# Two attention layers on one core: softmax denominators by 32x32 transposes and one product, another choice of moved sums, other buffers

## The chip, the core and the metric

The kernel runs on one core of a Trainium2 chip. Its engines have these names here: PE is TensorE (PEld its weight loads), DVE is VectorE, ACT is ScalarE, POOL is GpSimd, SP is SyncE, which only issues DMAs. The metric is the device time of one launch in microseconds (us), the median of several runs. Each engine works through its own queue of instructions in order, and waits on semaphores for the others.

## The reference

Two self-attention layers follow each other on `x` of shape (4, 64, 64, 256), that is 4 images of N = 4096 tokens with 256 channels. Everything is float32.

```python
# layer 0
q, k, v = x @ Wq + bq, x @ Wk + bk, x @ Wv + bv      # 32, 32 and 256 columns
x = gamma * (softmax(q @ k.T) @ v) + x               # softmax over the keys
# layer 1
f, g, v = x @ Wf + bf, x @ Wg + bg, x @ Wh + bh      # 32, 32 and 128 columns
o = softmax(g @ f.T) @ v
out = x + o @ Wo + bo
```

The kernel takes the exponentials without a maximum and divides by their sum at the end. The change is about that sum, the denominator of each token, in layer 1.

## The kernel before, in words

**Blocks and steps.** The work is a list of `Step(b, l, j, i)`: image b, layer l, block j of queries, step i over the keys. Layer 0 has 16 blocks of 256 queries with 8 steps of 512 keys; layer 1 has 8 blocks of 512 queries with 16 steps of 256 keys. Keys lie on the partitions, so a step's score tile `st` is 128 x 1024. One loop runs over all steps. In each, it issues the scores of the step after next (`later.scores()`), the DVE work of this step and the next, the products of this step, and small units of other work (`run(todo)`) that `plan` has put at fixed steps: projections of the next layer or image, and the `ends` of the block before. The tile framework then arranges the instructions of each engine by times of its own and adds the waits.

**One step.** ACT takes `p = exp(st)` (L544). Steps of layer 0 and the steps `SPLIT1` of layer 1 are split: ACT also makes `high` (L542), DVE makes `low` (L555) and `d` (L560), and PE multiplies each of the three with a part of v at one pass (L582, L600). The other steps of layer 1 multiply the whole `p`, which takes two passes (L600).

**Buffers.** Tiles of one tag share a number of buffers. `wide` makes 128 x 1024 tiles: tag `t` has two (`high`; in layer 1 also the `p` of split steps), `p` three, `l` two, `d` and `e` one each. `d` holds `d` in layer 0 and `p_sum` in layer 1. Tag `small` (128 x 256) has four and serves `x_res`, `x1`, `y` and two tiles of the start. Two PSUM tiles of tag `side` serve all small products: projections, transposes, outputs.

**Denominators of layer 0** come with the products, as a further column of v (W = C + 2).

**Denominators of layer 1.** `add_up` adds the `p` of a block's steps on DVE into `p_sum` (L571, L573), save those in `MOVED_SUMS`, which are added by DMA: the first is copied into `p_sum_moved` (tag `e`, L548), the others are accumulated there (L550), all issued from POOL's queue. `end_second` adds the two (L659), then its two halves (L660 `sums`, 128 x 512). The partitions are still to be summed: in each of the four units `output(t)`, PE takes 128 tokens of `sums` as the stationary operand and multiplies them with a column of ones (L668), beside the output product with Wo (L667) and into the same PSUM tile. DVE takes the reciprocal (L670), ACT scales the output by it (L673), and a DMA of POOL's queue accumulates it into `out` (L675). `plan` puts the four units at steps 1 to 4 of the next block.

**End of a block of layer 0.** `residual(s)`, for two tiles of 128 tokens: DVE makes `x1` (L628), SP writes it to `x1_dram`, POOL adds the last bias into `x_res` (L639), SP writes that to `out` (L640).

**Projections.** `qk_unit` multiplies the two parts of x into a PSUM tile `ps`. ACT copies its lower half into an SBUF tile `whole` (L439), DVE adds the upper half and the bias into `whole` (L440), ACT rounds it into `parts[top]` (L441), DVE takes the rest into `parts[bottom]` (L442), and SP writes `parts` to DRAM. `load_rows` (L493) loads queries and keys from there by POOL's queue; `keys` lists the loads still to come.

**The check at the end.** After the last block, DVE compares all reciprocals in `inverse` and the largest values in `seen_v` with bounds (L808 to L819), PE counts the violations (L821), and a branch (L831) would run a general path.

Of the kernel before, what the change touches and what calls it, by code (L numbers as in the profile page):

```python
# [57 lines left out]
P = 128  # L58
# [10 lines left out]
MOVED_SUMS = (0, 4, 7, 9, 12)  # L69
# [169 lines left out]
def fast_path(ctx: ExitStack, tc: tile.TileContext, x, w0, w1, wo, bo, gamma, out, off):  # L239
# [27 lines left out]
    def wide(tag, name, dtype=F32):  # L267
        return work.tile([P, 2 * QB], dtype, tag=tag, bufs={"d": 1, "e": 1, "p": 3}.get(tag, 2), name=name)
# [41 lines left out]

    inverse = const.tile([P, 2, B * N // P], F32, name="inverse")
# [12 lines left out]
    for l, (q_w, q_b, k_w, k_b, v_w, v_b) in enumerate((w0, w1)):  # L324
        queue = (nc.scalar, nc.gpsimd)[l]
        w_sb = work.tile([P, NCC, 2 * D], F32, tag="small", bufs=4, name=f"wqk_whole{l}")
        b_sb = const.tile([2 * D, 1], F32, name=f"bqk{l}")
        for g, w_dram, b_dram in ((0, q_w, q_b), (D, k_w, k_b)):
            queue.dma_start(w_sb[:, :, g : g + D], w_dram.rearrange("(c p) d -> p c d", p=P))
            queue.dma_start(b_sb[g : g + D, :], b_dram.rearrange("(d o) -> d o", o=1))  # L330
        w_parts = const.tile([P, NCC, 4 * D], F32R, name=f"wqk{l}")
        high, low = w_parts[:, :, : 2 * D], w_parts[:, :, 2 * D :]
        nc.scalar.copy(high, w_sb)
        nc.vector.tensor_sub(low, w_sb, high.bitcast(F32))
        wqk.append(w_parts)
        bqk.append(b_sb)
        v_sb = const.tile([P, NCC, CV[l]], F32, name=f"wv{l}")
        queue.dma_start(v_sb, v_w.rearrange("(c p) d -> p c d", p=P))
        wv.append(v_sb)
# [20 lines left out]
    def bias_units():  # L360


        def issue():
            nc.vector.tensor_scalar(bv, bv, gamma_sb, None, ALU.mult)
            wide_bias = work.tile([P, P], F32, tag="small", bufs=4, name="wide_bias")
# [10 lines left out]
    q_t, moved_sums, first_p, waiting = {}, {}, [], {}  # L376
# [35 lines left out]
    def project_units(b, l, h):  # L412
# [5 lines left out]
        def qk_unit():  # L418
# [10 lines left out]
            whole = data.tile([2 * D, QB0], F32, tag="qk", name=f"qk_{b}_{l}_{h}")  # L429
# [9 lines left out]
            nc.scalar.copy(whole, ps[bottom, :])  # L439
            nc.vector.scalar_tensor_tensor(whole, ps[top, :], bqk[l], whole, ALU.add, ALU.add)  # L440
# [50 lines left out]
    def load_rows(dst, parts, which, order):  # L491
        for n, h in enumerate(order):
            nc.gpsimd.dma_start(dst[n * D : (n + 1) * D, :], parts[h, which])  # L493
# [16 lines left out]
    def small(name):  # L510
        return work.tile([P, C], F32, tag="small", bufs=4, name=name)


    class Step:
# [8 lines left out]
        def scores(self):  # L523
# [19 lines left out]
            self.p = wide("t" if self.split and l == 1 else "p", f"p_{self.key}")  # L543
            nc.scalar.activation(self.p, s_flat, AF.Exp)  # L544
            if l == 1 and i in MOVED_SUMS:
                if i == MOVED_SUMS[0]:
                    moved_sums[b, j] = wide("e", f"p_sum_moved_{b}_{j}")
                    nc.gpsimd.dma_start(moved_sums[b, j], self.p)  # L548
                else:
                    nc.gpsimd.dma_start(moved_sums[b, j], self.p, accum_op=ALU.add)  # L550
# [13 lines left out]
        def add_up(self, p_sum):  # L564
# [5 lines left out]
            elif self.i == kept[1]:  # L570
                nc.vector.tensor_add(p_sum, first_p.pop(0), self.p)  # L571
            else:
                nc.vector.tensor_add(p_sum, p_sum, self.p)  # L573
# [80 lines left out]
    def end_second(b, j, acc, p_sum, o):  # L654
        key = f"{b}_{j}"
        for h in range(QB // QB0):
            nc.vector.tensor_add(o[h][:, :QB0], o[h][:, :QB0], acc[1][:, h * QB0 : (h + 1) * QB0])
        sums = work.tile([P, QB], F32, tag="sums", bufs=1, name=f"sums_{key}")
        nc.vector.tensor_add(p_sum, p_sum, moved_sums[b, j])  # L659
        nc.vector.tensor_add(sums, p_sum[:, :QB], p_sum[:, QB:])  # L660

        def output(t):
            def issue():
# [4 lines left out]
                nc.tensor.matmul(ps[:, C : C + 1], sums[:, tok], ones[:, :1], start=True, stop=True)  # L668
                n = (b * N + j * QB) // P + t
                nc.vector.reciprocal(inverse[:, 1, n : n + 1], ps[:, C : C + 1])  # L670
# [8 lines left out]
        return [output(t) for t in range(NT)]  # L679

    def run(units):
        for u in units:
            u()

# [15 lines left out]
    acc, p_sum, units = None, None, {}  # L700

    def plan(b, l, j, ends):
# [20 lines left out]
        else:  # L723
            for n, u in enumerate(ends):
                put(1 + n, u)
        if b + 1 < B:
# [8 lines left out]
    for n, s in enumerate(steps):  # L735
        b, l, j = s.b, s.l, s.j
        if s.first:
# [5 lines left out]
            if l == 1:  # L743
                p_sum = wide("d", f"p_sum_{b}_{j}")
# [24 lines left out]
        s.add_up(p_sum)  # L769
# [31 lines left out]
        if s.last:  # L801
            ends = end_first(b, j, acc) if l == 0 else end_second(b, j, acc, p_sum, o)
    run(ends)

    good = small("good").rearrange("p (l n) -> p l n", l=2)
    nc.vector.tensor_scalar(good, inverse, 1.0 / SUM_MAX, None, ALU.is_ge)  # L808
    nc.vector.tensor_scalar(inverse, inverse, 1.0 / SUM_MIN, None, ALU.is_le)
    nc.vector.tensor_mul(good, good, inverse)  # L810
    nc.vector.tensor_scalar(seen_v, seen_v, VALUE_MAX, None, ALU.is_le)
    size = const.tile([P, 1], F32, name="size")
    nc.vector.tensor_mul(size, gamma_sb, gamma_sb)
    nc.vector.tensor_scalar(size, size, GAMMA_MAX**2, None, ALU.is_le)
    low = const.tile([P, 1], F32, name="low")
    for seen, axes in ((good, AX.XY), (seen_v, AX.XY)):
        nc.vector.tensor_reduce(low, seen, axes, ALU.min)
        nc.vector.tensor_mul(size, size, low)
# [54 lines left out]
```

## Time and profile before

| What | Value |
|---|---|
| Median of 3 runs | 3158.69 us (3158.46 to 3160.62) |
| Profiled execution, its own time | 3155.92 us |
| Span of its profile | 3154.1 us |
| Granted TensorE clock | 0.998 |
| ACT: p (L544), 1024 times | 1042.5 us, 1021 ns each |
| DVE: low (L555), 704 times | 936.6 us, 1330 ns each |
| DVE: p_sum added (L573), 288 times | 352.6 us, 1224 ns each |
| DVE: transposes of x (L392), 112 times | 79.0 us, 705 ns each |
| PE: whole p (L600), 1280 passes | 611.0 us, 597 ns each |
| DMA: p into p_sum_moved, 160 issues | 512 KB each, 4.7 us to landing |

The page shows one execution. A row of a group gives line, engine, operation, what it writes and reads, shape, count, then busy time and mean duration, then the idle time of the engine just before and what ended it. Matmuls are pipelined and their ends are modelled, so on PE the distance from one start to the next says more than a duration. A row of the order in time gives start, duration, engine, line, operation, and how many were merged. "Passes" are PE instructions: a product of float32 operands is two of them, each with its own weight load; one of fp32r operands is one.

### The profile page before, as it was taken

To read this page: it belongs to the slowest core of one execution; us is meant where nothing else is said; L and a number is where in the kernel's file an instruction comes from. 1 tells how busy PE (TensorE), PEld (TensorE's weight loads), DVE (VectorE), ACT (ScalarE), POOL (GpSimd) and SP (SyncE) were. 2 spreads that over 40 slices of the span, in tenths; PEclk is the share of its full clock that TensorE was granted. 3 is DMA by queue.
4 is the path that set the end of the run, shared out by engine and by line. 5 is a ranking of instruction groups with operands and counts; after the bars stand their busy time and mean duration, and the time that the engine had idled before them with its cause. 6 is when DMAs were issued, how large, how long until landed. Compare 5 with 4: busy or idle time off the path is not lost.

```text
span 3154.1 us, 54090 instructions
## 1 busy us (share of the span) xinstructions
PE 3116.3 (99%) x19908; PEld 2672.0 (85%) x19908; DVE 2689.1 (85%) x3237; ACT 2140.1 (68%) x2835; POOL 900.7 (29%) x1108
## 2 busy tenths in 40 slices
PE   8999999999999999999999999999999999999997
PEld 7999998666799999866679999976668999996664
DVE  7888888888888888888888888898888888888876
ACT  7666666777666666777766666677776666666674
POOL 5232224222422222422242222232223222233221
PEclk9999999999999999999999999999999999999999
DMA  4121114555512121555541112255554111125454
GB/s 119 43 53 47 48 48 104 107 108 105 104 44 51 41 53 47 113 101 112 107 93 47 49 45 51 51 116 107 105 113 81 48 46 47 49 65 105 97 95 73
DMA packets 391392, 239.49 MB, mean 76 GB/s; under 512 B 266672, under 2 KB 355248, under 8 KB 391120
## 3 DMA queue, kind: packets, MB, share of 16 engines
q0 software_dynamic: 68160, 134.86, 22.0%
q1 hardware_dynamic: 322048, 100.76, 13.4%
q8 instruction: 161, 2.64, 0.4%
q14 instruction: 111, 0.91, 0.1%
q10 hardware_dynamic: 912, 0.33, 0.1%
HBM read 82.58 MB, written 67.11 MB: 47 GB/s over the span
## 4 chain that ended last, share of the span: by engine, by line
PE 91%; DVE 3%; DMA 2%; issue 2%; ACT 1%; POOL 0%; SPq 0%; DVEq 0%; ACTq 0%; POOLq 0%
PE acc L600 24%; PE acc L582 23%; PE acc_pair L582 23%; PE st L532 14%; PE psv L464 4%; PE psqk L422 2%; PE pso L667 2%; DVE d L560 1%; DVE low L555 1%; ACT p L544 1%; DVE p_sum L573 1%; DMA p_sum_moved<-p 0%; DMA squares<-in_x 0%; PE pso L668 0%; DMA squares<-x_dram 0%
## 5 line engine op out<-in xcount | busy, mean ns | idle before, releaser
L542 ACT ACTIVATE high<-st,down 128x1024 fp32r<-128x1024 f32 x704 | 786.5, 1117 | 703.2 <-PE st L532 362.8
L544 ACT ACTIVATE p<-st 128x1024 f32<-128x1024 f32 x1024 | 1042.5, 1021 | 166.3 <-PE st L532 143.8
L560 DVE SCALAR_TENSOR_TENSOR d<-low,high 128x1024 fp32r<-128x1024 f32 x704 | 871.0, 1237 | 227.0 <-PE acc_pair L582 223.7
L555 DVE TENSOR_TENSOR low<-p,high 128x1024 fp32r<-128x1024 f32 x704 | 936.6, 1330 | 142.6 <-ACT p L544 141.6
L532 PE MATMUL st<-q,k 128*128 128x256 f32 (+1 forms) x3072 | 706.3, 338 | 2.5 <-DMA k<-qk_parts 1.4
L600 PE MATMUL acc<-p,v 128*128 128x512 f32 x1280 | 611.0, 597 | 0.0
L532 PEld LDWEIGHTS st<-q,k 128*128 128x128 f32 x3072 | 470.0, 189 | 103.3 <-issue 40.6
L639 POOL TENSOR_TENSOR x_res<-x,bo 128x256 f32<-128x256 f32 x128 | 212.5, 1660 | 879.3 <-DVE x L628 879.2
L600 PEld LDWEIGHTS acc<-p,v 128*128 128x128 f32 x1280 | 233.1, 189 | 161.8 <-issue 143.4
L573 DVE TENSOR_TENSOR p_sum<-p_sum,p 128x1024 f32<-128x1024 f32 x288 | 352.6, 1224 | 9.4 <-ACT p L544 5.8
L582 PE MATMUL acc<-v0h,high 128*128 128x258 f32 x2048 | 341.6, 284 | 1.2 <-ACT high L542 1.2
L582 PE MATMUL acc<-v0d,d 128*128 128x258 f32 x2048 | 339.2, 287 | 2.6 <-DVE d L560 2.2
L582 PE MATMUL acc<-v0l,low 128*128 128x256 f32 (+1 forms) x2048 | 329.3, 283 | 0.6 <-DVE low L555 0.5
L582 PE MATMUL acc_pair<-v0h,high 128*128 128x258 f32 x2048 | 329.8, 283 | 0.0
L582 PE MATMUL acc_pair<-v0l,low 128*128 128x256 f32 (+1 forms) x2048 | 328.8, 282 | 0.0
L582 PE MATMUL acc_pair<-v0d,d 128*128 128x258 f32 x2048 | 328.5, 282 | 0.0
L582 PEld LDWEIGHTS acc<-v0h,high 128*128 128x128 f32 x2048 | 286.0, 189 | 3.1 <-issue 1.4
L582 PEld LDWEIGHTS acc<-v0d,d 128*128 128x128 f32 x2048 | 281.5, 190 | 5.6 <-DVE d L560 4.9
L582 PEld LDWEIGHTS acc<-v0l,low 128*128 128x128 f32 x2048 | 282.2, 190 | 1.8 <-DVE low L555 1.3
L582 PEld LDWEIGHTS acc_pair<-v0h,high 128*128 128x128 f32 x2048 | 282.1, 189 | 0.0
L582 PEld LDWEIGHTS acc_pair<-v0l,low 128*128 128x128 f32 x2048 | 281.1, 189 | 0.0
L582 PEld LDWEIGHTS acc_pair<-v0d,d 128*128 128x128 f32 x2048 | 281.0, 189 | 0.0
(108 smaller groups left out, 3332.5 us busy)
## 6 DMA issues: line engine op xcount, KB each, us to landing
p_sum_moved<-p POOLq DMA_DIRECT2D x160, 512.0 KB, 4.7
x_res<-in_x SPq DMA_DIRECT2D x128, 128.0 KB, 2.1
qk_dram<-qk_parts SPq DMA_DIRECT2D x128, 128.0 KB, 1.9
x_dram<-x SPq DMA_DIRECT2D x128, 128.0 KB, 1.7
out<-x_res SPq DMA_DIRECT2D x128, 128.0 KB, 1.7
squares<-x_dram SPq DMA_DIRECT2D x512, 32.0 KB, 1.9
out<-y POOLq DMA_DIRECT2D x128, 128.0 KB, 3.2
q<-qk_dram POOLq DMA_DIRECT2D x252, 64.0 KB, 2.2
```

The lines of the kernel that those rows point to most:

```text
L422: nc.tensor.matmul(ps, wqk[l][:, c, :], x_parts[key][n][:, c, :], start=(c == n == 0), stop=(c == NCC - 1 and n == 1),)
L464: nc.tensor.matmul(ps[:, t, :], xT[key][:, c, t * P : (t + 1) * P], wv[l][:, c, :], start=(c == 0), stop=(c == NCC - 1),)
L532: nc.tensor.matmul(st[:, g, :], k_t[b, l, kt // NT][:, kt % NT * P : (kt % NT + 1) * P], q_t[b, l, j * n // QB][:, q0 : q0 + n], start=Tru ...
L542: nc.scalar.activation(self.high, s_flat, AF.Exp, bias=down)
L544: nc.scalar.activation(self.p, s_flat, AF.Exp)
L555: nc.vector.tensor_sub(self.low, self.p, self.high.bitcast(F32))
L560: nc.vector.scalar_tensor_tensor(self.d, self.low.bitcast(F32), -UP, self.high.bitcast(F32), ALU.mult, ALU.add)
L573: nc.vector.tensor_add(p_sum, p_sum, self.p)
L582: nc.tensor.matmul(acc[2 * s + which][:, :width], p[:, g * QB0 + s * P : g * QB0 + (s + 1) * P], v0[self.i][v][:, g, :width], start=self.f ...
L600: nc.tensor.matmul(acc[which], v_part[:, g, :], p[:, g * QB : (g + 1) * QB], start=first and g == 0, stop=last and g == G[1] - 1,)
L639: nc.gpsimd.tensor_add(x_old[s], x_new[s], bo_sb)
L667: nc.tensor.matmul(ps[:, :C], part, wo_sb, start=True, stop=True)
```

## The change

Six edits stand in the diff.

1. **Denominators.** For all blocks of layer 1 but the very last, the four products with ones go. A unit `turn` transposes the 32x32 blocks of `sums` on DVE into the other half of `p_sum` and sums each run of 32, which gives `part_sums`, 128 x 16. A unit `denominators` multiplies it on PE with `same`, a constant with ones where two partitions agree modulo 32, into a side tile `psd` of 16 columns, and takes four reciprocals of 32 x 4. The two units stand ahead of the four outputs, so the ends of a block are six units, at steps 1 to 6 of the next. `same` is built on POOL at the start.
2. **Moved sums.** The steps are (3, 4, 6, 7, 9, 12) and not (0, 4, 7, 9, 12). The `p` of the first, step 3, is made in the tag-`e` buffer itself, so nothing is copied; five are accumulated there. `tc.issue_after(loads[0].ins)` keeps each behind the last load of `load_rows` in POOL's queue. `p_sum` is taken at the second kept step and no longer at the block's first.
3. **Buffers.** Tag `t` has three, `small` has three and not four, `sums` has no tile of its own.
4. **Projections.** `whole` stays in PSUM; the copy of the lower half lies in `parts[top]` until that is written.
5. **The order in `end_second`.** The moved sums are added before the output halves.
6. **The check** is split: all but the last block's four columns at step 13 of the last block, those four at the end.

```diff
-MOVED_SUMS = (0, 4, 7, 9, 12)
+MOVED_SUMS = (3, 4, 6, 7, 9, 12)
...
-        return work.tile([P, 2 * QB], dtype, tag=tag, bufs={"d": 1, "e": 1, "p": 3}.get(tag, 2), name=name)
+        return work.tile([P, 2 * QB], dtype, tag=tag, bufs={"d": 1, "e": 1, "p": 3, "t": 3}.get(tag, 2), name=name)
...
+    same = const.tile([P, P], F32, name="same")
+    nc.gpsimd.tensor_copy(same[:, :S], ident[:, :S])
+    for a in range(1, P // S):
+        nc.gpsimd.tensor_add(same[:, :S], same[:, :S], ident[:, a * S : (a + 1) * S])
+    for a in range(1, P // S):
+        nc.gpsimd.tensor_copy(same[:, a * S : (a + 1) * S], same[:, :S])
...
-            whole = data.tile([2 * D, QB0], F32, tag="qk", name=f"qk_{b}_{l}_{h}")
...
-            nc.scalar.copy(whole, ps[bottom, :])
-            nc.vector.scalar_tensor_tensor(whole, ps[top, :], bqk[l], whole, ALU.add, ALU.add)
+            whole, rest = ps[top, :], parts[top, :].bitcast(F32)
+            nc.scalar.copy(rest, ps[bottom, :])
+            nc.vector.scalar_tensor_tensor(whole, whole, bqk[l], rest, ALU.add, ALU.add)
...
-            nc.gpsimd.dma_start(dst[n * D : (n + 1) * D, :], parts[h, which])
+            loads[0] = nc.gpsimd.dma_start(dst[n * D : (n + 1) * D, :], parts[h, which])
...
-        return work.tile([P, C], F32, tag="small", bufs=4, name=name)
+        return work.tile([P, C], F32, tag="small", bufs=3, name=name)
...
-            self.p = wide("t" if self.split and l == 1 else "p", f"p_{self.key}")
+            base = l == 1 and i == MOVED_SUMS[0]
+            self.p = wide("e" if base else "t" if self.split and l == 1 else "p", f"p_{self.key}")
             nc.scalar.activation(self.p, s_flat, AF.Exp)
-            if l == 1 and i in MOVED_SUMS:
-                if i == MOVED_SUMS[0]:
-                    moved_sums[b, j] = wide("e", f"p_sum_moved_{b}_{j}")
-                    nc.gpsimd.dma_start(moved_sums[b, j], self.p)
-                else:
+            if base:
+                moved_sums[b, j] = self.p
+            elif l == 1 and i in MOVED_SUMS:
+                with tc.issue_after(loads[0].ins):
                     nc.gpsimd.dma_start(moved_sums[b, j], self.p, accum_op=ALU.add)
...
+        p_sum = p_sums[b, j]
+        nc.vector.tensor_add(p_sum, p_sum, moved_sums[b, j])
         for h in range(QB // QB0):
             nc.vector.tensor_add(o[h][:, :QB0], o[h][:, :QB0], acc[1][:, h * QB0 : (h + 1) * QB0])
-        sums = work.tile([P, QB], F32, tag="sums", bufs=1, name=f"sums_{key}")
-        nc.vector.tensor_add(p_sum, p_sum, moved_sums[b, j])
-        nc.vector.tensor_add(sums, p_sum[:, :QB], p_sum[:, QB:])
+        sums, squares = p_sum[:, :QB], p_sum[:, QB:]
+        nc.vector.tensor_add(sums, sums, squares)
+        n0 = (b * N + j * QB) // P
+        end = b == B - 1 and j == NQ[1] - 1
+        part_sums = work.tile([P, QB // S], F32, tag="part_sums", bufs=1, name=f"part_sums_{key}")
+        def turn():
+            nc.vector.transpose(squares, sums)
+            nc.vector.tensor_reduce(part_sums, squares.rearrange("p (n k) -> p n k", k=S), AX.X, ALU.add)
+        def denominators():
+            ps = side_psum(f"psd_{key}")[:, : QB // S]
+            nc.tensor.matmul(ps, same, part_sums, start=True, stop=True)
+            for a in range(P // S):
+                rows = slice(a * S, (a + 1) * S)
+                of_rows = ps[rows, :].rearrange("p (t a) -> p t a", a=P // S)[:, :, a]
+                nc.vector.reciprocal(inverse[rows, 1, n0 : n0 + NT], of_rows)
...
-                nc.tensor.matmul(ps[:, C : C + 1], sums[:, tok], ones[:, :1], start=True, stop=True)
-                n = (b * N + j * QB) // P + t
-                nc.vector.reciprocal(inverse[:, 1, n : n + 1], ps[:, C : C + 1])
+                n = n0 + t
+                if end:
+                    nc.tensor.matmul(ps[:, C : C + 1], sums[:, tok], ones[:, :1], start=True, stop=True)
+                    nc.vector.reciprocal(inverse[:, 1, n : n + 1], ps[:, C : C + 1])
...
-        return [output(t) for t in range(NT)]
+        return ([] if end else [turn, denominators]) + [output(t) for t in range(NT)]
...
+    def check(values):
+        good = wide("t", f"good_{values.shape[1]}")[:, : values.shape[1]]
...
+        nc.vector.tensor_scalar(good, values, 1.0 / SUM_MAX, None, ALU.is_ge)
+        nc.vector.tensor_scalar(values, values, 1.0 / SUM_MIN, None, ALU.is_le)
+        nc.vector.tensor_mul(good, good, values)
+        nc.vector.tensor_reduce(worst, good, AX.X, ALU.min)
+        nc.vector.tensor_mul(size, size, worst)
...
+        if (b, j) == (B - 1, NQ[1] - 1):
+            put(NI[1] - 3, check_all_but_last)
...
-    good = small("good").rearrange("p (l n) -> p l n", l=2)
-    nc.vector.tensor_scalar(good, inverse, 1.0 / SUM_MAX, None, ALU.is_ge)
...
-    for seen, axes in ((good, AX.XY), (seen_v, AX.XY)):
-        nc.vector.tensor_reduce(low, seen, axes, ALU.min)
-        nc.vector.tensor_mul(size, size, low)
+    check(in_last_block)
```

## The prediction

> **What bounds the kernel now.** I read the engine rows of the page first, then the waits of PE, then groups by form, then the order in time around the lines that change.
>
> ```profile
> PE 3116.3 (99%) x19908; PEld 2672.0 (85%) x19908; DVE 2689.1 (85%) x3237; ACT 2140.1 (68%) x2835; POOL 900.7 (29%) x1108
> ```
>
> ```profile
> PE count L821 <- DVE low L819: 4.8, 1, 4.8
> PE psqk L422 <- ACT xT L390: 3.7, 3, 1.5
> PE psx L389 <- DMA x_nat<-in_x: 3.7, 2, 3.3
> PE acc L582 <- DVE d L560: 2.2, 4, 0.8
> ```
>
> The second fence is from the waits of PE (total us, times, longest). All of it lies in the first 100 us, at the very end, or is small. A busy PE is not yet a full PE, so I added up its passes at their undisturbed spacing, start to start in the trace: 0.118 us for 256 or 258 columns of fp32r, 0.229 for 512, 0.429 for a pass of 512 fp32 columns, 0.215 for 256, 0.112 for the one-column product. That gives 3067 us of the 3140 between the first matmul (3.3) and the last (3143.3). About 25 of the missing 73 us lie before 150 us and about 9 at the end; the rest is about 0.5 in every 50 us, near the rounding of the spacings. So between 150 and 3110 us PE never really waits: **an instruction taken from PE is worth its spacing, and one taken from another engine nothing, unless PE comes to wait.**
>
> **What the Trainium skill says.** "TensorE: Matmul & The Clock Gate", § LDWEIGHTS (loading the stationary operand), makes the load depend on its columns, 128/1.2 = 107 ns; § Back-to-back issue gap adds that spacing is set by load and matmul together. The trace agrees: a product with one moving column still takes 0.112 us a pass. "VectorE: DVE Perf Modes", § The three transpose paths, says that VectorE transposes 32x32 blocks alone; L392 does that on 128x512 in 705 ns. "PSUM — Partial Sum Buffer", § Engine vs sequencer instructions: matmuls start in program order, so one that waits holds all behind it; in the trace no matmul overtakes another.
>
> **The denominators, on PE.** Groups by form, then the order in time on PE (start, us):
>
> ```profile
> L668 PE MATMUL pso<-ones,sums 128*128 128x1 f32 x256 | 36.2, 211 | 0.2
> L660 DVE TENSOR_TENSOR sums<-p_sum 128x512 f32<-128x512 f32 x32 | 21.8, 683 | 0.0
> ```
>
> ```profile
> 571.22 0.28 PE L668 MATMUL pso<-ones,sums 128*128 128x1 f32 x2
> 571.36 1.96 PE L600 MATMUL acc<-p,v 128*128 128x512 f32 x4
> 572.76 1.03 PE L600 MATMUL acc<-d,v 128*128 128x512 f32 x2
> 573.63 0.62 PE L532 MATMUL st<-q,k 128*128 128x512 f32 x2
> 574.09 0.28 PE L422 MATMUL psqk<-xh,wqk 128*128 128x256 f32 x1
> ...
> 577.68 1.88 PE L600 MATMUL acc<-p,v 128*128 128x512 f32 x4
> 578.99 1.03 PE L600 MATMUL acc<-d,v 128*128 128x512 f32 x2
> 579.86 0.63 PE L532 MATMUL st<-q,k 128*128 128x512 f32 x2
> 580.33 1.88 PE L600 MATMUL acc<-p,v 128*128 128x512 f32 x4
> ```
>
> The same four whole, two d and two score passes take 580.33 - 577.68 = 2.65 us without L668 and 574.09 - 571.22 = 2.87 with it. So one denominator product (two passes) costs PE 0.22 us although it moves one column; its two loads do it. Of 128 such products 124 go (the last block keeps four): -124 x 0.223 = -27.7. The 31 products psd come in. They have 16 moving columns and the same two loads, and are not in the trace: 0.22 each by the nearest row, bounds 0.2 to 0.3: +31 x 0.223 = +6.9. **Net -20.7 on the path.**
>
> **The denominators, on DVE.** Per block a transpose (0.60 from start to start, as L392 and L660 have it when something follows) and a tensor_reduce of 512 elements come in. L817 takes 420 ns for 256 and 286 for 128, so 0.69 for 512, about 0.62 of spacing. Reciprocals stay four per block. One p_sum add of 1.14 goes with the sixth moved step: 10 instead of 11 steps are kept, so 9 adds instead of 10. Sum about +0.1 per block: nothing, at 88% DVE busy (219.8 of 250 us, stretch 545:795). What counts is when psd and its readers are ready. Let E be the end of a block's last product into acc[1].
> - Blocks with projections of the next image (21 of the 31): PE reaches psd at E + 6.65 (scores 0.46, high and low 0.92, scores 0.46, q and k 0.47, a whole step 1.72, d 0.46, scores 0.46, a whole step 1.72). DVE does two o adds (0.33 each, from 0.1), sums 0.60, d 1.14, transpose 0.60, then low of step 3, which cannot start before ACT's two exponentials of that step, about E + 4.05, then the reduce: done at E + 5.9. Ahead by 0.8. Then pso_0 takes psd's side buffer, free after the reciprocals, which stand behind 0.40 + 1.14 + 0.34 + 1.14 of other DVE work: E + 9.3, where PE arrives at E + 9.1. A wait of 0 to 0.28; I take 0.14, so +2.9.
> - Last image (7 blocks): the reduce stands ahead of that low, ready at E + 3.9; PE comes at E + 4.5. Nothing.
> - End of layer 1 with another image behind it (3): d of layer 0 needs p_sum's buffer, which is now held past the reduce. psd about 0.4 late and d 0.5 late; the trace has about 0.6 of stall there already. The third high buffer lets PE do the high products of step 2 meanwhile. Net +1.0 in all (0 to 4).
>
> **Other edits.** Moved sums: 160 DMAs as before, the plain copy replaced by a fifth accumulate. They go one after the other (4.7 us to land, median): step 12's lands about 19 us after step 6's exponential, its add comes at about 24. A late one would hold a p buffer and then ACT; today ACT waits 10.2 us in all for them. Behind the loads of keys on POOL: a load waits for a score product of an earlier step than the sum's own exponential, so the sum waits for nothing new: 0, bounds -2 to +3. Small, four buffers to three: the second x1 now takes the first x1's place. In the trace the second L628 starts 2.83 us after the first ends, while the add L639 ends at 1.83 and the write to x1_dram lands at 1.73: covered by 1.0; without that cover 64 blocks would wait. The fourth y waits for the first y's landing (3.2 us), about three steps later: covered. Third high buffer: only ACT waits for it now, so 0 for PE, up to -3. Projections kept in PSUM: the side buffer is freed about 0.9 later (end of L442, not L440). In the first 50 us the next user is psx, whose reader on ACT then comes some 0.1 late per unit: +1.0 (0 to 4). The new constant lies on POOL between 7.8 and 12.0 us, where POOL waits for the first keys: 0.
>
> **The tail.** Order in time:
>
> ```profile
> 3138.50 0.17 DVE L670 RECIPROCAL inverse<-pso 128x1 f32<-128x1 f32 x1 [0.49 <-PE pso L668]
> ...
> 3140.65 0.29 DVE L808 TENSOR_SCALAR good<-inverse 128x256 f32<-128x256 f32 x1 [1.99 <-DMA out<-y]
> ...
> 3143.00 0.15 DVE L819 TENSOR_SCALAR low<-size 128x1 f32<-128x1 f32 x1
> ```
>
> good waited 1.99 us for a y buffer to land, and seven instructions followed. Now it lies in a t buffer and six instructions on four columns remain, at about 0.19: done at 3139.85 in place of 3143.16, -3.3. The last y lands at 3143.4, next in line, and the branch behind the flag takes three us anyway; I take -3.0 (0 to -3.3). The larger part of the check (about 2 us of DVE) lies in the last block, where DVE is 80% busy: 0.
>
> **Sum.** -20.7 - 3.0 + 2.9 + 1.0 + 1.0 = -18.8. The profiled execution took 3155.92 (span 3154.1), so 3137.1; the median of the runs shown is 2.8 above it: **3139.9, rounded 3140.**
>
> **Rivals.**
> - More than forecast: no new wait shows, and the buffers take up some of the 25 us at the start. -20.7 - 3.3 - 3 = -27: 3131.7. For it: PE hardly waits anywhere. Against: the starting chain runs through ACT and DVE. Chance 0.12.
> - Half of it: the bounds of the waits come true, 21 x 0.28 + 4 + 4 = 13.9, tail 0: -6.8: 3151.9. Chance 0.14.
> - Nothing to be told: a free PE runs into DVE, 88% busy in layer 1, which then sets the pace in 21 blocks by about 0.8 us each, +17: -5: 3153.7. Chance 0.09.
> - Slower, one mechanism: psd holds PE's queue behind the reduce, the reduce behind low of step 3, and that behind ACT's L544. Waits of low for L544 exist (141.6 us in 145 times, longest 2.6). I count ACT 0.8 ahead; were it 2.6 late in 21 blocks, psd would cost 21 x (2.6 - 0.8) = 38: 3158.7 - 24 + 38 = 3173. It decides from 1.1 us of wait per such block (break even; ACT 1.9 later than counted) and is measurable as slower from 1.4. Against it: 145 waits are spread over 704 lows, mean 1.0. Chance 0.05.
> - That the products stay in place is excluded by the instructions: 31 psd and 4 with ones are left.
>
> **The numbers.** Likeliest case 0.60, between -12 and -25. A change of 0.2% (6.3 us) is about what a measurement can tell. Faster 0.60 + 0.12 + 0.14 = 0.86; same 0.09; slower 0.05. The range 3133 to 3150 leaves out the low rival's end and the three high ones' greater part, 0.2 in all.
>
> **What would show it.** Right: PE 19722 passes, psd at 0.22 of spacing, no wait of PE for part_sums or inverse over 5 us in all, reduce at 0.69, L808's wait for out gone. Wrong: PE's loads waiting for part_sums by a microsecond per block, x1 or y waiting for DMAs on DVE or ACT with PE idle behind them, or more than 30 us idle before 150.

## The result, and the profile after

The changed kernel takes **3170.15 us** (median of 5 runs, 3168.74 to 3175.18) against 3158.46 for the kernel before on the same chip: ratio **1.0043, 95% interval 1.003 to 1.0056**. It is slower by 12 us where 19 us of gain were forecast. Its profiled execution took 3170.15 (span 3168.3), 14.2 above that of before.

The engine row of its page, then four rows of the waits of PE (total us, times, longest us):

```profile
PE 3111.7 (98%) x19722; PEld 2654.3 (84%) x19722; DVE 2689.9 (85%) x3272; ACT 2129.8 (67%) x2835; POOL 882.3 (28%) x1115
```

```profile
PE psqk L430 <- ACT xh L413: 12.1, 8, 2.8
PE acc L593 <- DVE d L570: 4.4, 8, 1.1
PE count L863 <- DVE low L861: 3.4, 1, 3.4
...
PE st L540 <- DMA k<-qk_dram: 2.5, 1, 2.5
```

The passes fell from 19908 to 19722, as the diff says. But PE's busy time fell by 4.6 us only, and the span grew: PE now waits. The first row is new. In the kernel before, PE waited once, for 0.7 us, for `xh`, the high part of the turned x.

To see where, I set the sum of all passes at their undisturbed spacing (the spacings of the prediction) against the time from the first to the last matmul. What is left over is **idle**. "Starts of layer 1" is the sum over the four images of the 50 us from 1 us before layer 0's last product; "layer 1 to 0" is three times the 50 us from 8 us before the next image's first layer-0 product; "end" is what lies past 3090 us. All in us:

| Kernel | Passes | Idle | Before 150 us | Starts of layer 1 | Layer 1 to 0 | Other | End |
|---|---|---|---|---|---|---|---|
| before | 3067.3 | 72.7 | 27.2 | 4.0 | 4.8 | 29.4 | 7.3 |
| changed | 3046.5 | 106.5 | 32.1 | 25.4 | 10.0 | 32.6 | 6.6 |

So the 20.8 us of passes are gone, just as counted, and 33.8 us of idle came in their place, 21.4 of them at the four starts of layer 1. The remaining 1.2 lie behind the last matmul.

This is PE in order of time at the first of these starts (start us, duration us, engine, line, operation; in brackets the wait before it and its releaser):

```profile
558.63 0.70 PE L611 MATMUL acc<-low,v 128*128 128x512 f32 x2
562.14 0.58 PE L430 MATMUL psqk<-xh,wqk 128*128 128x256 f32 x1 [2.81 <-ACT xh L413]
562.52 1.91 PE L472 MATMUL psv<-wv,xT 128*128 128x256 f32 x4
...
564.44 0.41 PE L430 MATMUL psqk<-xh,wqk 128*128 128x256 f32 x1
564.65 0.41 PE L430 MATMUL psqk<-xl,wqk 128*128 128x256 f32 x1
```

PE stands 2.8 us before the first projection of the next image. (The fourth image has no next one: there PE stands before the scores of step 14, the `st` row of 2.5 us above.) Then something else shows: two `psqk` passes start 0.21 us apart, where 0.118 is usual. The stretches say why (us, PE busy, granted clock, DMA share, GB/s):

```profile
555.00:562.00 7.00, 4.33 (x15) 0.96 0.51 104
562.00:568.00 6.00, 5.86 (x17) 0.50 0.54 97
600.00:606.00 6.00, 6.00 (x24) 1.00 0.56 100
```

**After the wait PE runs at half its clock for some 6 us** (0.50 from 562 to 568). The wait is paid a second time. In the four images the waits were 2.98, 2.97, 2.98 and 2.64 us from start to start beyond the spacing, and in the 10 us behind them PE took 3.1, 1.8, 1.8 and 2.5 us more than the spacings of its passes (0.8 of the last is one more wait, for `p`). The Trainium skill ("TensorE: Matmul & The Clock Gate", § What's actually happening) gives half rate after an idle window of about 3.4 us; here waits of 2.6 to 3.0 us were followed by it. Not every such wait is: in e4 below PE waited 2.9 us here in the third image, and the clock stayed at 1.00.

What PE waits for is found by going back along VectorE (here from the end of layer 0's last block; same columns):

```profile
529.62 1.22 DVE L584 TENSOR_TENSOR p_sum<-p,p 128x1024 f32<-128x1024 f32 x1
...
532.61 0.48 DVE L639 SCALAR_TENSOR_TENSOR x<-o,g,x_res 128x256 f32<-128x256 f32 x1
533.00 1.22 DVE L584 TENSOR_TENSOR p_sum<-p_sum,p 128x1024 f32<-128x1024 f32 x1
534.14 0.48 DVE L448 SCALAR_TENSOR_TENSOR psqk<-psqk,bqk,qk_parts 64x256 f32<-64x256 f32 x1
534.53 1.35 DVE L570 SCALAR_TENSOR_TENSOR d<-low,high 128x1024 fp32r<-128x1024 f32 x1
535.81 0.47 DVE L639 SCALAR_TENSOR_TENSOR x<-o,g,x_res 128x256 f32<-128x256 f32 x1
...
559.60 1.22 DVE L570 SCALAR_TENSOR_TENSOR d<-low,high 128x1024 fp32r<-128x1024 f32 x1
560.73 0.71 DVE L400 STREAM_TRANSPOSE xT<-squares 128x512 f32<-128x512 f32 x1
```

and the same place before:

```profile
524.74 0.49 DVE L628 SCALAR_TENSOR_TENSOR x<-o,g,x_res 128x256 f32<-128x256 f32 x1
525.23 1.23 DVE L571 TENSOR_TENSOR p_sum<-p,p 128x1024 f32<-128x1024 f32 x1
526.37 0.97 DVE L628 SCALAR_TENSOR_TENSOR x<-o,g,x_res 128x256 f32<-128x256 f32 x1
```

There is a **chain** that the prediction never followed. (A unit is 256 tokens, an image has 16.) The last two x1 of layer 0 are written to DRAM; eight DMAs read them back as 32x32 squares; VectorE turns them (unit 15 of layer 1); PE projects them; that frees the buffer into which eight more DMAs load the next image's unit 0, which is turned and projected in turn. A second branch writes unit 15's keys to DRAM and loads them for the scores of step 14. In the changed kernel PE waits on the first branch in three images, on the second in the fourth. Measured from the last layer-0 product (third image, us):

| | x1 first, second | write issued | unit 15 loads begin | turned | unit 0 of next image turned | PE reaches its product, undisturbed | begins |
|---|---|---|---|---|---|---|---|
| before | 3.3, 5.0 | 6.1 | 8.2 | 16.6 | 27.2 | 30.35 | 30.8 |
| changed | 5.0, 8.2 | 8.7 | 12.2 | 19.5 | 32.0 | 29.9 | 33.45 |

PE can begin 1.4 us after that second transpose starts (32.0 to 33.45). Before, this left 1.7 us to spare (30.35 - 27.2 - 1.4); now the transpose is 4.8 us later. Two delays are in the fence above: an add to `p_sum` now stands ahead of both x1 (529.62; it stood between them), and the second x1 comes 3.2 us after the first, not 1.6. With three small buffers it takes the first one's, and VectorE's list has an add, a `psqk` and a `d` ahead of it. VectorE does not stand idle for the buffer there: in three of the images the first one's write had landed some 0.9 us before. The third delay is the write of the second x1, which lands after 3.4 us in three of the images, not after 1.75; the loads begin less than 0.1 us behind that landing.

### The profile page after: what moved, and what is told of

Read it like the earlier page. It is cut to its first block, busy times and chain, and to the rows that moved or that the text cites. A ratio compares the mean times of both kernels' runs of the same rounds, so it can differ in the third digit from the quotient of the medians.

```text
span 3168.3 us, 53630 instructions
## 1 busy us (share of the span) xinstructions
PE 3111.7 (98%) x19722; PEld 2654.3 (84%) x19722; DVE 2689.9 (85%) x3272; ACT 2129.8 (67%) x2835; POOL 882.3 (28%) x1115
## 4 chain that ended last, share of the span: by engine, by line
PE 85%; DMA 4%; issue 4%; DVE 3%; ACT 2%; POOL 1%; SPq 1%; DVEq 0%; POOLq 0%; ACTq 0%
PE acc L593 22%; PE acc_pair L593 22%; PE acc L611 21%; PE st L540 13%; PE psv L472 5%; PE psqk L430 2%; DMA p<-p 1%; PE pso L696 1%; DVE d L570 1%; DMA out<-y 1%; DMA squares<-x_dram 1%; SPq L280 1%; DVE low L565 1%; ACT p L554 1%; POOL k L501 0%
## 5 line engine op out<-in xcount | busy, mean ns | idle before, releaser
L584 DVE TENSOR_TENSOR p_sum<-p_sum,p 128x1024 f32<-128x1024 f32 x256 | 312.0, 1219 | 20.4 <-ACT p L554 17.6
L560 POOL DMA_DIRECT2D p<-p x160 | 142.6, 891 | 639.9 <-ACT p L554 294.7
```

The source lines that it names most:

```text
L584: nc.vector.tensor_add(p_sums[self.b, self.j], so_far, self.p)
```

## The experiments

All runs compare with the kernel before on the same chip, so ratios are used; each ratio's interval reaches at most 0.0016 to either side. The changed kernel stands at 1.0043.

**One edit undone or moved, first round.** The first three go back to two `t` buffers, since a fourth small buffer or the tile `qk` does not fit beside three.

```diff
 e1: -"p": 3, "t": 3}
     +"p": 3}
 e2: e1, and
     -tag="small", bufs=3
     +tag="small", bufs=4
 e3: e1, and
     -whole, rest = ps[top, :], parts[top, :].bitcast(F32)
     -nc.scalar.copy(rest, ps[bottom, :])
     -nc.vector.scalar_tensor_tensor(whole, whole, bqk[l], rest, ALU.add, ALU.add)
     +whole = data.tile([2 * D, QB0], F32, tag="qk", ...)
     +nc.scalar.copy(whole, ps[bottom, :])
     +nc.vector.scalar_tensor_tensor(whole, ps[top, :], bqk[l], whole, ALU.add, ALU.add)
```

> One edit to the changed kernel: the tag t has two buffers again in place of three; everything else as changed. It also is the base of two other runs, since a fourth small buffer or the old tile for projections fits beside two t buffers only. Theory A (the 24 us of new idle at the four starts of layer 1 come from the three small buffers: the second x1 of the last layer-0 block waits for the first one's write, its turned tokens come late, PE waits for unit 15 and for the next image's unit 0, and runs at half its clock after the longer waits): no effect on the idle there; 3168 to 3174 us, within 4 of the changed kernel. Theory B (the sums of steps 0, 1 and 2, now kept, stand ahead of x1 on VectorE): the same, no effect. Theory C (the third t buffer reorders the scheduler's list so that VectorE's transposes of layer 1 stand behind d): the idle at the starts of layer 1 goes, 3146 to 3152 us.

> The run before and one more edit: four small buffers in place of three. Theory A (small buffers): the second x1 of the last layer-0 block follows the first within 2.0 us instead of 3.2, PE's waits for xh at the starts of layer 1 go, and with them the half clock: 3146 to 3153 us, 15 to 24 below the run with two t buffers and three small ones; out<-y has a shorter queue as well. Theory B (kept sums ahead of x1): x1 comes 1.2 us earlier only, of 2.7; half of the idle stays: 3158 to 3166 us. Theory D (projections kept in PSUM hold side buffers and so delay the chain): no change, 3168 to 3174 us.

> The run with two t buffers and one more edit: the projection of q and k goes to a tile of its own in SBUF again (tag qk), as in the kernel before, so that its side buffer is released by the first of VectorE's two instructions. Theory D (side buffers held longer): PE's waits for xh in the first 150 us fall from 12 to below 5 us, idle there by 5 us, and the starts of layer 1 lose part of their waits: 3150 to 3164 us. Theories A and B: only the first 150 us change, by 0 to 5 us: 3163 to 3172 us.

Measured: e1 **1.0108**, e2 **1.0062**, e3 **1.0095**. No theory expected e1: without the third buffer the kernel is 20 us slower still. The idle came in ordinary blocks (other 49.4, from 32.6), not at the starts (25.8). The fourth small buffer gives 14.6 us back, though not where theory A had it: starts 26.5, other 40.6, end 6.0. The tile `qk` gives 4.8 us, before 150 us (27.7 of idle, from 33.4), as the second half of its expectation said. In e2 the second x1 follows the first by 0.39 us; but both come at 6.9 and 7.3, behind both first adds to `p_sum`, and on SP's queue the loads stand behind the write of `qk_parts` and begin at 12.0 to 12.5, so the chain is as late as ever. PE's waits for `xh` fell from 9.8 us (e1) to 2.9, but it now waits 7.8 us in four times for unit 15's keys, the second branch. Taking away one delay does not free the chain. Which branch PE meets first differs between the programs; it is the keys in e2, e4, e7, e9, e10, e12, e13 and e17.

**The adds behind x1.** The order of tracing in steps 1 and 2 of the first block:

```diff
-        s.add_up()
         todo = units.get(s.i, [])
+        residual_first = l == 1 and j == 0 and s.i in (1, 2)
+        if not residual_first:
+            s.add_up()
...
             run(todo)
+            if residual_first:
+                s.add_up()
```

> The changed kernel with one edit in the order of tracing: in steps 1 and 2 of the first block of layer 1 of each image the add to p_sum is traced behind the two residual units (x1 and its write) and not ahead of them. Buffers as in the changed kernel. Theory B (kept sums ahead of x1): x1_0 comes 1.1 us earlier and x1_1 by 1.1 to 2.3, the turned tokens follow, and the idle at the four starts of layer 1 falls from 24 to below 8 us: 3150 to 3158 us. Theory A (small buffers): the wait of x1_1 for the write of x1_0 stays, half of the idle or more stays: 3158 to 3170 us. Theory C: no change, 3168 to 3172 us.

Measured: **1.0038**, not to be told from 1.0043. x1 comes at 3.4, the second at 7.1, behind another add (from 6.0), although the first one's write had landed at 5.6. The starts keep 21.0 of 25.4.

**More time for the chain.**

```diff
-put(6 * n, t), put(6 * n + 2, qk), put(6 * n + 3, v)
+at = 8 * n
+put(at, t), put(at + 2, qk), put(at + 3, v)
...
-i = 12 + 7 * h - j * NI[1]
+i = 14 + 7 * h - j * NI[1]
```

> The changed kernel with the projections in layer 1 planned two steps later: unit 15 from step 6 to 8, and the units of the next image from 12 + 7h to 14 + 7h. In the trace of the changed kernel PE comes to the next image's unit 0 3.5 to 4.6 us before its turned tokens are there, after a chain of x1, its write, eight loads of squares, the transpose, unit 15's product on PE, eight loads again and a transpose, that had about 2 us of slack before. Two steps are 5.3 us. Theory A (the chain is late by what several small edits took from it, and PE's wait and the half clock behind it are its whole price): the idle at the four starts of layer 1 falls from 24 to below 6 us: 3148 to 3155 us. Theory B (the waits come from VectorE being full at these places, and a later plan only moves them): 3164 to 3173 us.

Measured: **1.0032**, starts 26.7. The edit did not do what it says: unit 15's product moved by six passes, that of the next image's unit 0 not at all. It stands 115 passes behind layer 0's last one in both built programs, since the order of each engine's list is worked out when the program is built and doesn't follow the tracing here. So this run tells nothing about theory A.

**Single parts on the kernel before, and the denominators undone in the changed one.** e6 takes `same`, `turn`, `denominators`, the late `p_sum` and the order in `end_second` into the kernel before; e7 takes `MOVED_SUMS` and the base in `e`; e8 restores the products with ones in the changed kernel.

```diff
 e8: -return ([] if end else [turn, denominators]) + [output(t) for t in range(NT)]
     +return [output(t) for t in range(NT)]
     (and the product with ones and its reciprocal for every block)
```

> The kernel before with one part of the change alone: denominators by transpose, reduce and psd. Moved sums (0, 4, 7, 9, 12) by copy and adds, two t buffers, four small ones, projections in their own tile and the check at the end as before. Theory A (the denominators are worth the passes they take from PE; the losses lie in the other edits): 20.7 us of passes less, 0 to 5 us of new waits: 3138 to 3144 us. Theory B (transpose and reduce at the block's start hold VectorE, and with two t buffers ScalarE and PE wait at each block's start, as the 24 us between two and three t buffers say): 3150 to 3165 us.

> The kernel before with one part of the change alone: moved sums (3, 4, 6, 7, 9, 12), the first of them kept in the buffer e instead of copied; not traced behind loads of keys; buffers and denominators as before. Theory A (the kept sums of steps 0, 1 and 2 ahead of x1 on VectorE, and the transfers of steps 4 and 6 beside the write of x1, eat the slack of the chain at the starts of layer 1): x1 1 to 2 us later there, PE waits for the next image's unit 0 in three images, 3164 to 3180 us. Theory B (they change nothing, as the prediction had it): 3156 to 3161 us. Theory C (one add less on VectorE helps): below 3156 us.

> The changed kernel with its denominators undone alone: every block has its four products of sums with ones and four reciprocals again, no transpose, no reduce, no psd; all else as changed. Theory A (the denominators are worth 20.7 us of passes and cost 3 us of waits): 3186 to 3192 us. Theory B (they cost waits of about the size of their gain, through VectorE at the starts of blocks): 3165 to 3178 us. In both the idle at the starts of layer 1 stays at 20 us or more, since nothing of the denominators stands there.

Measured: e6 **1.0003** (0.9994 to 1.0011), e7 **1.0092**, e8 **1.0115**. The new moved steps alone cost 29 us: idle at the starts 33.5, nearly everything else as before. Theory A of e7 had the cause, but not the size (at most 3180 us; 3185 were measured) nor the branch: PE waits for unit 15's keys in all four images, not for the next image's unit 0 in three.

```profile
PE st L532 <- DMA k<-qk_dram: 15.5, 4, 5.2
```

In e7 both x1 come at 6.9 and 7.3, behind two adds (from 2.9 and 4.2), and the loads at 12.0 to 12.7, on SP's queue behind the write of `qk_parts`. In three of the images x1's two writes land after 1.7 to 2.1 us, about as before, so there the moved transfers did not hold them up.

The denominators alone, on the kernel before, bring nothing: passes 3046.5, but idle 92.4, the 19.7 more lying in ordinary blocks (other 42.3) and layer 1 to 0 (10.9). In the changed kernel they are worth 22.7 us. A difference between the two places is seen on ACT. The waits of ACT for `t` buffers (`high` is the first write into one, and VectorE's `low`, `d` and `p_sum` are its last readers); before, then e6:

```profile
ACT high L542 <- DVE low L555: 141.9, 102, 1.8
...
ACT high L542 <- DVE d L560: 20.3, 17, 2.0
```

```profile
ACT high L549 <- DVE low L562: 156.6, 114, 1.8
...
ACT high L549 <- DVE d L567: 55.3, 40, 4.4
```

In the changed kernel, with a third buffer, the first of these rows is gone and the second is small:

```profile
ACT high L550 <- DVE d L570: 2.2, 2, 1.1
```

**The square of four.** With e16 the two edits are seen with and without each other.

> The changed kernel with both the denominators and the third t buffer undone: products with ones again, two t buffers. With the runs that undid one of them it makes a square of four: changed 1.0043, two t buffers 1.0108, products with ones 1.0115. Theory A (the third buffer is worth its 20 us only where the passes are taken from PE, since before that the waits for t are hidden behind PE): 1.0105 to 1.0135, the same as with ones and three t buffers. Theory B (the third buffer takes up the delays of the new moved steps and of the small buffers, with or without the denominators): 1.016 to 1.020.

Measured: **1.0151**.

| | three `t` buffers | two |
|---|---|---|
| psd | 1.0043 (changed) | 1.0108 (e1) |
| ones | 1.0115 (e8) | 1.0151 (e16) |

The third buffer is worth 20 us with psd and 11 with ones; psd is worth 23 us with three buffers and 14 with two. The expectations had 0 or all of it; it lies between. So even with the products with ones the waits for `t` were not all hidden, at least beside the other edits. Three `t` buffers with psd on the kernel before were not tried: that those waits make the 19.7 us of e6 is argued, not shown.

**The first block, all blocks, the starting stretch.** e9 and e10 set the moved steps back; e11 sends the first image's layer-0 projections through `e`; e12 is e9 and e11.

```diff
 e9:  +MOVED_FIRST = (0, 4, 7, 9, 12)
      +self.moved = MOVED_FIRST if j == 0 else MOVED_SUMS
 e10: -MOVED_SUMS = (3, 4, 6, 7, 9, 12)
      +MOVED_SUMS = (0, 4, 7, 9, 12)
      +moved_sums[b, j] = wide("e", ...)      # filled by a copy of p
 e11: +if b == l == 0:
      +    whole = wide("e", f"qk_{h}")[: 2 * D, :QB0]
      +    rest = whole
      ...
      -nc.vector.scalar_tensor_tensor(whole, whole, bqk[l], rest, ALU.add, ALU.add)
      +nc.vector.scalar_tensor_tensor(whole, ps[top, :], bqk[l], rest, ALU.add, ALU.add)
```

> The changed kernel, but in the first block of layer 1 of each image the moved sums are those of steps 0, 4, 7, 9, 12, the first of them kept in the buffer e (free there); the other seven blocks as changed. Three t buffers, three small ones. The changed kernel stands at 1.0043 of the kernel before. Theory A (the choice of moved steps costs its time in the first block of layer 1 alone, where the chain from x1 to the next image's unit 0 has about 2 us to spare): no wait over 1 us of PE for xh there, 15 to 24 us gone: 0.9965 to 0.9998 of before, 3145 to 3155 us. Theory B (the three small buffers cost it): x1_1 still waits for the write of x1_0, half of the idle stays: 1.001 to 1.003. Theory C (third t buffer or side buffers held longer): 1.003 to 1.005.

> The changed kernel with the moved sums of the kernel before in every block: (0, 4, 7, 9, 12), the first by a copy into e; still traced behind the loads of keys. Theory A: as the run with the first block's steps alone, but one add of 1.1 us more for VectorE in each block and a transfer at each block's start: 0 to 10 us above that run: 0.997 to 1.002 of before. Theory B (small buffers): 1.001 to 1.004. If the new steps help nowhere, the two runs agree within 0.001.

> The changed kernel, but the projections of q and k of the first image's layer 0 (the starting stretch) go through a piece of the buffer e, which is free there, in place of PSUM; all later ones stay in PSUM. Theory A (side buffers held longer cost the starting stretch 5 us and nothing else): 4 to 6 us below the changed kernel, 1.0024 to 1.0031 of before. Theory B (the 5 us at the start are due to the order on ScalarE, or to GpSimd's new constant): no change, 1.0040 to 1.0046.

> Both edits on the changed kernel: old steps in the first block of layer 1, first projections through e. Theory A: the gains add up, 20 to 29 us below the changed kernel: 0.995 to 0.998 of before, 3143 to 3151 us, faster than both. Theory B (small buffers): 0.9995 to 1.002.

Measured: e9 **1.0024**, e10 **1.0005**, e11 **1.0014**, e12 **1.0001**. e9 falls into theory B's range: the starts keep 16.9 us, and the second x1 still comes at 6.0. e10 is 6 us below e9, so the new steps do not pay in the other seven blocks together either. e11 takes the idle before 150 us from 32.1 to 27.3; its ratio fell by 0.0029 (9 us), the idle by 6.4; with the intervals of the two ratios the 5 us of theory A are not excluded. None of the four frees the chain: with the old steps (e9, e10, e12) the first x1 comes at 2.4, but the second, in the first one's buffer, at 6.0 to 6.1, behind an add (from 4.9).

**x1 without a small buffer.** x1 is computed in place over `o`, which is free anyway until the next block's end.

```diff
-x_new[s] = small(f"x1_{key}_{s}")
+x_new[s] = o[s][:, :C]
```

e13 is this alone, e14 adds e10 and e11, e15 adds e9 and e11 instead.

> The changed kernel with one edit: x1 is written in place over o (of which it is computed) and takes no small buffer, so that nothing of x1 waits for a small buffer, and the three small ones serve x_res and y alone. Theory A (the chain at the start of layer 1 lost its slack to several edits, the wait of x1_1 for the write of x1_0 among them): x1_1 follows x1_0 within 1.7 us in place of 3.2, the squares of unit 15 are loaded 2 us earlier, PE's waits over 1 us at the four starts shrink from about 6 to about 3 us each: 0.9998 to 1.0025 of before (changed kernel: 1.0043). Theory B (only the kept sums ahead of x1 matter): no change, 1.0035 to 1.0050. Theory C (small buffers alone): all idle at the starts gone, 0.996 to 0.998.

> The changed kernel with three edits: x1 in place over o, the moved sums of the kernel before in every block, the first projections through the buffer e. Kept are the denominators by transposes, the third t buffer, the check in the last block. Theory A (the chain at the starts of layer 1, and the starting stretch, are where the gain of the denominators went): the chain has its old slack again, idle at the starts below 2 us each: 0.993 to 0.997 of before, 3134 to 3147 us, faster than both. Theory B (x1's buffer doesn't matter): 0.998 to 1.0005, as the run with both earlier edits.

> As the run before, but with the old moved steps in the first block of layer 1 alone, and the new ones in the other seven. Theory A: 0.993 to 0.998; if the new steps cost elsewhere too, as the 6 us between the two earlier runs say, 2 to 6 us above the run with old steps everywhere. Theory B: 0.998 to 1.001.

Measured: e13 **1.002**; e14 **0.9945 (0.9931 to 0.9958)**, 3143.38 us against 3160.79; e15 **0.9957**. **e14 is faster than both kernels**, by 17 us than the one before. Alone, neither the buffer (e13, starts 22.6) nor the steps (e10, starts 16.0) frees the chain; together they do (starts 8.1, idle 82.1 in all). VectorE in e14 at this place, then PE, then the clock:

```profile
523.82 0.88 DVE L644 SCALAR_TENSOR_TENSOR o<-o,g,x_res 128x256 f32<-128x256 f32 x2
```

```profile
551.27 0.70 PE L616 MATMUL acc<-low,v 128*128 128x512 f32 x2
551.81 0.28 PE L430 MATMUL psqk<-xh,wqk 128*128 128x256 f32 x1
```

```profile
552.00:558.00 6.00, 5.78 (x24) 1.00 0.87 155
```

Both x1 follow each other at once, 2.3 and 2.7 us behind layer 0's last product. The transposes come at 15.0 and 27.1, and PE goes from its products to the next image's projection with no wait, at full clock. In the third and fourth image it still waits 1.5 and 1.3 us for unit 15's keys, at full clock too. x1 in place on the kernel before was not tried, so how the gain of e14 over that kernel divides is not shown; its starts had 4.0 us of idle to give.

**Which part of the new steps, and the tie on GpSimd.** e17 is e13 with the order of e4. e18 is e14 without `issue_after`.

> The changed kernel with two edits: x1 in place over o, and in steps 1 and 2 of the first block of layer 1 the adds to p_sum traced behind the residual units. The new moved steps stay. Theory A (what the new steps take from the chain is the add ahead of x1): x1_0 and x1_1 both by 4.2 us after the end of layer 0's products, no wait over 2 us at the four starts: 0.997 to 0.9995 of before. Theory B (it is the transfers of steps 4 and 6, which run beside x1's write and the loads of squares, and the fuller VectorE in steps 5 to 14): 1.0005 to 1.0025, as with x1 in o alone.

> The run with x1 in place, old steps and the first projections through e, less one more part of the change: the moved sums on GpSimd are no longer tied behind the loads of keys. Theory A (a load waits for nothing that the sum does not wait for, as the prediction had it): 0.9938 to 0.9952 of before, the same as with the tie. Theory B (the tie lets the last keys go first and keeps PE's scores of step 14 from waiting): 0.996 to 1.000.

Measured: e17 **0.9985 (0.9978 to 0.9992)**, starts 11.9; e18 **0.9951 (0.9937 to 0.9964)**. So it is the place of the adds for the greater part: with the new steps kept, their order alone is worth 11 us once the buffer is out of the way (e13 to e17), and nothing that can be told while it is not (e4). But the edit does two things at once. The second x1 comes only 0.5 us earlier than in e13 (6.0; by 4.2 was expected), and its write is issued at 6.5, ahead of the first moved transfer (8.1), and lands after 1.7 to 2.8 us; in e13 it is issued at 7.6, behind that transfer (7.1), and lands after 3.0 to 4.7. How much of the 11 us is VectorE's and how much the write's (theory B of e17) is not shown. 4 us of idle more than in e14 stay. The tie behind the loads of keys does nothing that can be told.

## Why the prediction was wrong, step by step

The sum forecast -18.8 in the profiled execution; +14.2 was measured. The 33 us between them:

- **Passes of PE: right.** -20.8 for -20.7. The reduce takes 676 ns (0.69 forecast). psd was put at 0.22 of spacing; from its first pass to the next product's it takes 0.14 in 21 blocks and 0.21 to 0.24 in ten, within 2 us of the count.

```profile
L680 DVE TENSOR_REDUCE part_sums<-p_sum 128x16 f32<-128x512 f32 x31 | 21.0, 676 | 0.4
L685 PE MATMUL psd<-part_sums,same 128*128 128x16 f32 x62 | 10.0, 237 | 0.2
```

- **psd and pso_0 in the blocks: the sum right by luck, its parts not.** +2.9 forecast; the "other" idle rose by 3.2. In the 21 blocks with projections psd was to be ready 0.8 ahead and pso_0 to wait 0.14 each; PE waited 3.1 us in all before psd and 1.5 before pso_0, most of it in seven of these blocks. In the last image, where nothing was forecast, psd waited 1.0. The rival that psd holds PE's queue is not what made it slower, though the sign it was given came true.
- **Moved sums, "0 (-2 to +3)": the largest failure.** They cost 29 us alone on the kernel before (e7), and undoing them in the changed one gives 12 us back (e10). The step looked at the DMAs, their landing and the p buffers. It did not follow which *adds* the new choice leaves: keeping steps 0, 1 and 2 puts an add on VectorE ahead of x1 in the one block per image where x1 starts a chain with 1.7 us to spare. Steps that are no longer moved had no term in the sum.
- **Small, four to three, "covered by 1.0": failed.** The cover was read from the distance of two x1 in the common layer-0 blocks (2.83 us from end to start), and there it held (2.84 after). In the last block before layer 1 they stood 1.6 us apart from start to start; with three buffers they stand 3.2 apart or more, with other work of VectorE between. Alone this hides behind the adds, and the adds behind this (e4, e9, e10 and e13 against e14 and e17).
- **Third t buffer, "0 (to -3)": mis-sized.** It is worth 20 us here (e1), a gain, so it does not explain the loss: the rest of the change would have lost more without it. The likely reason, argued from e6 and the square of four, is that ACT's 142 us of waits for `low` were in part hidden behind PE as long as PE had its passes. The rival "nothing to be told: a free PE runs into DVE" fits e6, the kernel without the buffer: 19.7 us of new idle, +17 in the rival.
- **Starting stretch, +1.0 (0 to 4): too small.** +4.9, by the projections in PSUM: e3 and e11 each take 5 us of idle away there.
- **Layer 1 to 0, +1.0 (0 to 4): too small.** +5.2. The wait of `acc` for `d` (4.4 us in 8 times; 2.2 in 4 before) is what was foreseen. No run took that buffer apart, so the rest of it is not shown.
- **Tail, -3.0: less than half.** From the last add to `p_sum` to the count 8.7 us pass, 10.0 before: -1.3.

```profile
3153.06 0.17 DVE L725 TENSOR_SCALAR good<-inverse 128x4 f32<-128x4 f32 x1
3155.17 0.17 DVE L726 TENSOR_SCALAR inverse<-inverse 128x4 f32<-128x4 f32 x1 [1.94 <-ACT y L703]
```

The step moved `good` away from the small buffers, but not `inverse`: L726 overwrites what the fourth y still reads as its scale, and that y waited 1.78 us for the landing of an earlier one, with three small buffers.

By idle, the miss is 21.4 at the starts, 3.9 and 4.2 in the two stretches that were too small, and 3.5 at the end with what follows the last matmul.

## What to carry to other kernels

A cover must be read at the place where it is thinnest: an instruction that repeats 64 times may start a long chain of DMAs in only four of them, and those four decide. A move of work shows its price in what stays behind as much as in what goes. When passes are taken from the engine that bounds the kernel, look at the waits of the others for buffers: what was hidden by just that amount is next, and one edit that seems worth nothing (a third buffer) may be what lets another one count.

## What the runs showed of the hardware

- In the changed kernel each of the four waits of PE of 2.6 to 3.0 us was followed by a granted clock of 0.50 to 0.53 over 3 to 6 us (1.00 in undisturbed stretches). Waits of 11.6 us in all cost some 8 us more. In e4 a wait of 2.9 us was followed by 1.00.
- A product with 16 moving columns in float32, of two passes, took 0.14 us of PE's time in 21 of 31 cases, where one of a single column takes 0.22.
- A 128 x 256 write to DRAM (the second x1) that landed after 1.75 us in the kernel before took 3.4 at the same place in three images of the changed one, and 3.0 to 4.7 in e13, with a 512 KB moved sum issued 0.5 to 1.6 us before it. In e17, where it goes out 1.6 us ahead of that transfer, it took 1.7 to 2.8. That the transfer is the cause is not shown.
